# Hawk and RWKV layer on one core: three groups of entries moved in a hand-written order table

## The chip, the cores and the metric

The kernel runs on one core of one Trainium2 chip. The metric is the device time of one execution in microseconds (us). Shown times are the median of three runs; the profile is of one further execution.

## The reference

For 8 sequences of 1024 tokens and 256 channels, in float32, a block adds a recurrent layer (Hawk) and a channel mix (RWKV) to its input. Both read the normalised input.

```python
xn = layernorm(x)                                  # over the 256 channels
# Hawk, 384 hidden channels
gate, u = xn @ Wg.T, xn @ Wi.T
y = causal_depthwise_conv(u, conv_w) + conv_b      # 4 taps
ig = sigmoid(y @ lru_Wi.T + lru_bi)
rg = sigmoid(y @ lru_Wg.T + lru_bg)
alpha = exp(-8 * softplus(lam) * rg)
xbeta = sqrt(1 - alpha**2 + 1e-6) * ig * y
h = scan(h[t] = alpha[t] * h[t-1] + xbeta[t])
hawk = (gelu(gate) * h) @ Wo.T
# RWKV channel mix; x_prev is xn one token earlier
xr = mu_r * xn + (1 - mu_r) * x_prev
xk = mu_k * xn + (1 - mu_k) * x_prev
rwkv = sigmoid(xr @ W_r.T) * (relu(xk @ W_k.T)**2 @ W_v.T)
out = x + hawk + rwkv
```

## The kernel before

The kernel goes through the 8 sequences in 8 rounds, one sequence a round, with the work of neighbouring sequences laid over each other: while a round's matrix products run, the next sequence is normalised, turned and mixed, and the sequence before has its recurrence finished. All products are in float32 on tiles of 128 rows by 512 tokens (or, for r, v and o, four blocks of 128 tokens).

**Products in groups.** A pair of row blocks times two halves of the tokens would be four outputs of two products each. The class `Group` makes them with seven products in place of eight, from sums of weight blocks (`sum_u`, `sum_l`, ... made once on POOL, line 408) and differences of token halves (`xsum`, `ysum`, `rsum`, ... made each round on POOL, line 797). A group uses PSUM banks named A, B, C (and D where there is a third channel block) and runs in numbered steps on TensorE (lines 415 and 421):

- step 1: a product into A, one into C. ScalarE then copies A into B (`seed`, line 491) and C into an SBUF tile (`five`, line 496).
- step 2: A is completed and evicted as output (0,0); a product is added into B. VectorE then writes B + five into C (`fork_c`, line 499).
- step 3: a product is added into B, one into C. VectorE then writes B + five as output (1,1), for groups without a third block straight into the output's place (`fork_d`, line 507), followed by `late`, ScalarE's function on it in place; for the groups l into bank D. C is evicted as output (0,1).
- step 4: a last product is added into B, which needs fork d to have read B first; B is evicted as output (1,0). Step 5, with a third block only, completes D.

The groups are u0, u1, u2 (both input projections), l0, l1, l2 (both gates' projections of y), k, r, v, o. Their evictions differ: u goes to `u` by a copy (line 611) or to `g` by Gelu (line 615); l to `tr` and `ti` by Tanh (line 623); k by Relu (line 660) and, once both rows of a token half are there, Square (line 663) into the tile `ysum`, which is lent to the key; r by Tanh into `side` (line 675).

**The first round** differs: its first group is plain, v is four plain products with the key's squares (`v_product`, line 824) whose results VectorE multiplies with r (`value`, line 846), and the second sequence is normalised in it. For that, VectorE takes statistics of x (line 721 and 723, "second stats"), ScalarE takes the root (`deviation`, line 726, which needs a table of its own), VectorE the reciprocal and the scaled mean (`inverse`, lines 733 and 734), and ScalarE normalises eight tiles (`normalize`, line 743), which TensorE turns (line 748). VectorE also runs nine convolution steps (`conv_rest`, line 880), three for each third of `y`. The group l0 needs the thirds of y and, from POOL, the differences `ysum` of their halves.

**The second round** has at its end the statistics of the sequence after next (`stats`, lines 721 and 723). They read `xt`, which four DMAs on SP's queue fill (`load_for_squares`, line 717), issued behind sixteen DMAs that turn the normalised tiles into `xnT` (`spread`, line 786). VectorE there also finishes the mixed inputs `xk` and `xr` of the next sequence (`mix`, line 814; ScalarE has started them in `mix_before`, line 808), two channel blocks each. Of the mixed key POOL makes token differences into `side`.

**The order.** No scheduler is at work. TensorE's steps are called in the order wanted (`pe`, which advances a clock by the product count). All else is put down with `at`, whose time comes from the table `PLACES` where the step's name stands in it. At the end everything is sorted by time and issued in that order; each engine works through its own instructions strictly in it:

```python
        if name in places:
            t = base[0] + places[name]
        steps.append((t, len(steps), f, args, name))
...
        for _, _, f, args, _ in sorted(steps, key=lambda e: e[:2]):
            f(*args)
```

`PLACES` has one table for the first round, one for the second, one for the rounds in the middle and one for the last. Its numbers are counted in TensorE products from the round's start; only their order has an effect. A step's name is the group's, the function's and its arguments: "k evict B 1 0" is the key's eviction of bank B, "deviation" and "inverse 0 8" in the first table are the second sequence's root and scales, "mix k 1" is channel block 1 of the mixed key.

Of the kernel before, what the change touches and what calls it, by code (L numbers as in the profile page):

```python
# [60 lines left out]
        "u1 late": 27.8, "conv_rest 1 1": 28.18, "r five": 28.48, "conv_first 2": 29.16,  # L61
        "early token_sum r 1": 29.68, "u2 evict B 1 0": 30.51, "conv_rest 0 1": 30.84,
        "u1 evict B 1 0": 31.19, "u2 late": 31.87, "early token_sum r 2": 32.34, "k fork_d": 32.34,
        "early constant 2": 33.49, "early token_sum r 3": 33.63, "r fork_c": 33.77, "deviation": 33.9,
        "early constant 3": 34.38, "early weight_sum l 3 False": 34.51, "k evict B 1 0": 34.53,
        "inverse 0 8": 35.4, "early weight_sum l 2 False": 35.77, "r fork_d": 35.86, "k late": 36.28,
        "conv_rest 2 1": 36.43, "normalize 7 1": 36.67, "early weight_sum o 0 False": 37.83,
        "conv_rest 1 2": 38.21, "r evict B 1 0": 39.35, "early weight_sum v 2 False": 39.7,
        "k evict C 0 1": 40.03, "conv_rest 0 2": 40.08, "early weight_sum o 1 False": 41.29,
        "r evict A 0 0": 41.42, "conv_rest 0 3": 41.48, "r evict C 0 1": 42.02, "normalize 1 1": 42.7,  # L70
        "conv_rest 2 2": 42.96, "normalize 4 1": 43.4, "normalize 6 1": 44.1, "token_sum y 0": 44.45,
        "r late": 44.8, "normalize 2 1": 45.47, "conv_rest 1 3": 45.6, "l0 seed": 46.8,
        "conv_rest 2 3": 47.0, "l0 five": 47.65, "normalize 5 1": 48.29, "value 0": 48.34,
        "token_sum y 1": 48.34, "normalize 0 1": 48.93, "value 6": 49.06, "token_sum y 2": 49.38,
        "l0 evict A 0 0": 49.72, "value 2": 49.8, "normalize 3 1": 50.52, "token_sum y 3": 50.52,
        "l0 fork_c": 50.86, "value 4": 51.67, "early weight_sum v 0 False": 51.68, "l1 seed": 51.86,
# [55 lines left out]
        "v evict B 1 0": 57.82, "token_sum y 1": 57.82, "mix_before r 0": 57.85, "o evict C 0 1": 58.55,  # L132
        "mix_before r 1": 58.96, "token_sum y 3": 59.0, "token_sum y 2": 60.16, "l0 evict A 0 0": 60.18,
        "l0 fork_c": 60.36, "v late": 61.32, "token_sum x 0": 62.12, "l1 seed": 62.36,
        "token_sum x 2": 63.28, "l1 five": 63.36, "stats 7 1": 63.74, "token_sum x 1": 64.44,
        "l0 fork_d": 64.47, "stats 6 1": 65.28, "add_x": 65.61, "mix k 1": 66.01,
        "l0 evict C 0 1": 66.36, "decay 0": 67.3, "stats 0 1": 67.5, "token_sum x 3": 67.5,
        "stats 4 1": 68.23, "l0 evict B 1 0": 68.64, "mix k 0": 68.96, "decay_square 0": 69.44,
        "mix r 0": 70.46, "l1 evict A 0 0": 70.55, "token_sum k 0": 71.96, "l1 fork_c": 71.96,
# [1196 lines left out]
```

## Time and profile before

| what | value |
|---|---|
| median of 3 runs | 624.31 us (623.81 to 625.08) |
| the profiled execution: time | 624.13 us |
| the profiled execution: span from first to last instruction | 622.4 us |
| granted TensorE clock over the span | 1.00 |
| share of the chain that ended last: TensorE | 93% |
| same chain: VectorE, ScalarE, DMA | 3%, 2%, 1% |

Times inside the profile are counted from the start of the span. PE is TensorE's products, PEld its weight loads, DVE is VectorE, ACT is ScalarE, POOL is GpSimd, SP the queue that issues most DMAs. A row of the timeline gives start, duration, engine, line, operation, out<-in by the program's names, partitions by elements, the number of instructions run together, and in brackets the engine's idle time before them with what ended it. A row of the waits gives who waited, for whom, the sum in us, how often and the longest. A second name behind a bank tile says which operands: w_r,xr are the products of r. Instructions that follow on VectorE and ScalarE without a wait start about 0.1 us before the row ahead of them ends.

### The profile page before, as it was taken

The page shows a single profiled execution, that of the slowest core. Times are in us where ns is not written, and L with a number is a line of the kernel's source. Part 1 is how long each engine was busy: PE and PEld are TensorE (multiplying, and loading weights), DVE is VectorE, ACT ScalarE, POOL GpSimd, SP SyncE. Part 2 cuts the span into 40 slices and gives each one's busy share as a digit, 9 for nine tenths or more (in the row PEclk, how much of TensorE's full clock was granted, in tenths as well). Part 3 has the DMA queues.
Part 4 walks back from the last instruction along what each step waited for, and adds up shares of the span by engine and source line. Part 5 has one row for each costly group of instructions (what it writes and reads, how often), then busy time and mean ns, then how long its engine had stood idle before and what let it go on. Part 6 is the DMA issues. An engine that isn't in the chain of part 4 may idle for free.

```text
span 622.4 us, 7477 instructions
## 1 busy us (share of the span) xinstructions
PE 613.1 (99%) x2539; PEld 369.8 (59%) x2539; DVE 530.4 (85%) x656; ACT 473.1 (76%) x670; POOL 321.6 (52%) x227
## 2 busy tenths in 40 slices
PE   8999999999999999999999999999999999999997
PEld 4566445954459544695447844487445964457466
DVE  5788699989889898897889988998888987789695
ACT  4997998658985689847889398884888749883880
POOL 4996743667225870449506493084911769427000
PEclk9999999999999999999999999999999999999999
DMA  7200600064001730029000390006600044000403
GB/s 271 67 2 10 127 0 1 22 182 67 1 0 39 179 55 0 1 60 198 14 1 1 77 194 0 2 2 141 130 0 1 18 118 70 0 0 1 69 20 115
DMA packets 35334, 35.10 MB, mean 56 GB/s; under 512 B 2784, under 2 KB 34784, under 8 KB 35296
## 3 DMA queue, kind: packets, MB, share of 16 engines
q1 hardware_dynamic: 26560, 25.83, 15.1%
q0 software_dynamic: 8320, 8.39, 9.1%
q8 instruction: 20, 0.33, 0.2%
q10 hardware_dynamic: 416, 0.41, 0.2%
q14 instruction: 18, 0.15, 0.1%
HBM read 19.94 MB, written 8.39 MB: 46 GB/s over the span
## 4 chain that ended last, share of the span: by engine, by line
PE 93%; DVE 3%; ACT 2%; DMA 1%; issue 1%; DVEq 0%; ACTq 0%
PE bank L415 62%; PE bank L421 24%; PE bank L824 4%; PE bank L1007 1%; PE bank L581 1%; DMA out_dram<-side 1%; DVE q L897 1%; DVE xk L814 0%; DVE xr L814 0%; DVE st L721 0%; ACT g L615 0%; PE bank L748 0%; DVE bank L499 0%; PE bank L1026 0%; ACT L726 0%
## 5 line engine op out<-in xcount | busy, mean ns | idle before, releaser
L415 PE MATMUL bank<-y,w_l 128*128 128x512 f32 x288 | 137.9, 593 | 0.0
L880 DVE SCALAR_TENSOR_TENSOR y<-u,par,y 128x1024 f32<-128x1024 f32 x72 | 111.4, 1572 | 0.2
L491 ACT COPY bank<-bank 128x512 f32<-128x512 f32 x76 | 43.7, 576 | 62.4 <-PE bank L415 46.5
L415 PEld LDWEIGHTS bank<-y,w_l 128*128 128x128 f32 x288 | 53.0, 190 | 58.6 <-issue 57.3
L499 DVE TENSOR_TENSOR bank<-bank,five 128x512 f32<-128x512 f32 x76 | 52.3, 689 | 27.1 <-PE bank L415 25.5
L415 PE MATMUL bank<-ysum,sum_l 128*128 128x512 f32 x144 | 71.1, 593 | 0.2 <-DVE bank L499 0.2
L415 PE MATMUL bank<-xsum,sum_u 128*128 128x512 f32 x138 | 69.3, 592 | 0.0
L797 POOL TENSOR_TENSOR tr<-g 128x512 f32<-128x512 f32 x12 | 22.0, 1835 | 79.9 <-ACT u L611 69.3
L797 POOL TENSOR_TENSOR ysum<-y,ysum 128x512 f32<-128x512 f32 x16 | 28.5, 1779 | 52.4 <-DVE y L880 52.3
L797 POOL TENSOR_TENSOR xsum<-ysum 128x512 f32<-128x512 f32 x12 | 16.0, 1350 | 66.0 <-PE bank L421 58.8
L415 PEld LDWEIGHTS bank<-ysum,sum_l 128*128 128x128 f32 x144 | 26.9, 190 | 35.0 <-issue 28.2
L496 ACT COPY five<-bank 128x512 f32<-128x512 f32 x76 | 43.7, 583 | 5.1 <-PE bank L415 3.2
L415 PE MATMUL bank<-xnT,w_u 128*128 128x512 f32 x92 | 47.0, 592 | 0.0
L623 ACT ACTIVATE tr<-bank,half_b 128x512 f32<-128x512 f32 x48 | 32.1, 680 | 17.2 <-PE bank L415 17.2
L415 PEld LDWEIGHTS bank<-xsum,sum_u 128*128 128x128 f32 x138 | 25.7, 190 | 29.7 <-issue 27.5
L421 PE MATMUL bank<-w_o,g 128*128 128x128 f32 x288 | 37.0, 275 | 0.0
L623 ACT ACTIVATE ti<-bank,half_b 128x512 f32<-128x512 f32 x48 | 31.5, 683 | 7.1 <-PE bank L415 6.9
L421 PEld LDWEIGHTS bank<-w_o,g 128*128 128x128 f32 x288 | 35.0, 192 | 2.9 <-issue 2.9
L743 ACT ACTIVATE xt<-xt,mv,std 128x256 f32<-128x256 f32 x60 | 34.0, 596 | 1.7 <-DVE mv L734 1.7
L904 DVE SCALAR_TENSOR_TENSOR ti<-ti,y 128x1024 f32<-128x1024 f32 (+1 forms) x25 | 31.0, 1259 | 3.9 <-ACT ti L623 3.9
L797 POOL TENSOR_TENSOR ysum<-y 128x512 f32<-128x512 f32 x16 | 21.3, 1329 | 23.8 <-DVE y L880 23.8
L907 DVE SCALAR_TENSOR_TENSOR ti<-ti,q 128x1024 f32<-128x1024 f32 (+1 forms) x25 | 32.6, 1305 | 0.7
(164 smaller groups left out, 1476.7 us busy)
## 6 DMA issues: line engine op xcount, KB each, us to landing
side<-in_x_dram POOLq DMA_DIRECT2D x8, 1024.0 KB, 9.3
xt<-in_x_dram SPq DMA_DIRECT2D x28, 256.0 KB, 4.5
xnT<-xk SPq DMA_DIRECT2D x96, 64.0 KB, 2.0
out_dram<-side SPq DMA_DIRECT2D x12, 512.0 KB, 5.0
xt<-in_x_dram SPq DMA_DIRECT2D x1, 1024.0 KB, 5.5
out_dram<-side SPq DMA_DIRECT2D x4, 256.0 KB, 2.2
out_dram<-side SPq DMA_DIRECT2D x8, 128.0 KB, 1.7
w_l<-in_lru_wg_dram SPq DMA_DIRECT2D x1, 576.0 KB, 5.9
```

The lines of the kernel that those rows point to most:

```text
L415: nc.tensor.matmul(banks[b], weight, tokens, start=start, stop=True, skip_group_check=True)
L421: nc.tensor.matmul(banks[b][:, p], tokens[:, p], weight, start=start and j == 0, stop=True, skip_group_check=True,)
L491: nc.scalar.copy(banks[bank["B"]], banks[bank["A"]])
L496: nc.scalar.copy(self.five, banks[bank["C"]])
L499: nc.vector.tensor_tensor(banks[bank["C"]], banks[bank["B"]], self.five, ALU.add)
L623: nc.scalar.activation(dst[:, m, HALVES[h]], src, AF.Tanh, bias=half_b[:, b + m : b + m + 1], scale=0.5)
L743: nc.scalar.activation(xa, xa, AF.Identity, bias=m, scale=r)
L797: nc.gpsimd.tensor_tensor(dst[o], a, b, ALU.subtract)
L824: nc.tensor.matmul(banks[b][:, j * D : (j + 1) * D], lhs[:, c, (t + j) * P : (t + j + 1) * P], families[w][:, c, :], start=(j == 0 and c = ...
L880: nc.vector.scalar_tensor_tensor(y[:, m, :], u[:, m, k : k + S], column(COL_CONV_W + k * HC + m), y[:, m, :], ALU.mult, ALU.add,)
L904: nc.vector.scalar_tensor_tensor(ti[:, m, p], ti[:, m, p], 1.0, y[:, m, p], ALU.add, ALU.mult)
L907: nc.vector.scalar_tensor_tensor(ti[:, m, p], ti[:, m, p], 0.5, q[:, m, p], ALU.mult, ALU.mult)
```

## The change

Nothing is added and nothing left out. Entries of the table get other numbers, and so other places among the instructions of their engines.

First round: `deviation` goes from 33.9 to 40.1 and `inverse 0 8` from 35.4 to 41.0. On ScalarE the root, with the two table loads around it, so moves behind the key's eviction of B with its square, the key's late relu, r's eviction of B, and the key's eviction of C with its square. On VectorE the reciprocal and the scaled means move behind r's fork d and three of the convolution steps. `normalize 7 1`, `2 1` and `6 1` move with them: the first tile is normalised behind r's evictions of A and C, three others a little later than before.

Second round: `l0 fork_d` goes from 64.47 to 63.7 and `mix k 1` from 66.01 to 64.0, `stats 7 1` from 63.74 to 64.5. On VectorE fork d and mix k 1 so move ahead of `stats 7 1` and `stats 6 1`.

TensorE's, POOL's and SP's instructions keep their order, and so do the tables of the other rounds.

```diff
@@ table "first" @@
-        "early constant 2": 33.49, "early token_sum r 3": 33.63, "r fork_c": 33.77, "deviation": 33.9,
+        "early constant 2": 33.49, "early token_sum r 3": 33.63, "r fork_c": 33.77,
-        "inverse 0 8": 35.4, "early weight_sum l 2 False": 35.77, "r fork_d": 35.86, "k late": 36.28,
-        "conv_rest 2 1": 36.43, "normalize 7 1": 36.67, "early weight_sum o 0 False": 37.83,
-        "conv_rest 1 2": 38.21, "r evict B 1 0": 39.35, "early weight_sum v 2 False": 39.7,
-        "k evict C 0 1": 40.03, "conv_rest 0 2": 40.08, "early weight_sum o 1 False": 41.29,
-        "r evict A 0 0": 41.42, "conv_rest 0 3": 41.48, "r evict C 0 1": 42.02, "normalize 1 1": 42.7,
-        "conv_rest 2 2": 42.96, "normalize 4 1": 43.4, "normalize 6 1": 44.1, "token_sum y 0": 44.45,
-        "r late": 44.8, "normalize 2 1": 45.47, "conv_rest 1 3": 45.6, "l0 seed": 46.8,
-        "conv_rest 2 3": 47.0, "l0 five": 47.65, "normalize 5 1": 48.29, "value 0": 48.34,
+        "early weight_sum l 2 False": 35.77, "r fork_d": 35.86, "k late": 36.28, "conv_rest 2 1": 36.43,
+        "early weight_sum o 0 False": 37.83, "conv_rest 1 2": 38.21, "r evict B 1 0": 39.35,
+        "early weight_sum v 2 False": 39.7, "k evict C 0 1": 40.03, "conv_rest 0 2": 40.08,
+        "deviation": 40.1, "inverse 0 8": 41.0, "early weight_sum o 1 False": 41.29,
+        "r evict A 0 0": 41.42, "conv_rest 0 3": 41.48, "r evict C 0 1": 42.02, "normalize 7 1": 42.6,
+        "normalize 1 1": 42.7, "conv_rest 2 2": 42.96, "normalize 4 1": 43.4, "token_sum y 0": 44.45,
+        "r late": 44.8, "conv_rest 1 3": 45.6, "l0 seed": 46.8, "conv_rest 2 3": 47.0, "l0 five": 47.65,
+        "normalize 2 1": 47.7, "normalize 6 1": 48.0, "normalize 5 1": 48.29, "value 0": 48.34,
...
@@ table "second" @@
-        "token_sum x 2": 63.28, "l1 five": 63.36, "stats 7 1": 63.74, "token_sum x 1": 64.44,
-        "l0 fork_d": 64.47, "stats 6 1": 65.28, "add_x": 65.61, "mix k 1": 66.01,
+        "token_sum x 2": 63.28, "l1 five": 63.36, "l0 fork_d": 63.7, "mix k 1": 64.0,
+        "token_sum x 1": 64.44, "stats 7 1": 64.5, "stats 6 1": 65.28, "add_x": 65.61,
```

## The prediction

> **What bounds the kernel now.** The page's busy row came first, then the waits of TensorE, then the timeline around the two longest.
>
> ```profile
> PE 613.1 (99%) x2539; PEld 369.8 (59%) x2539; DVE 530.4 (85%) x656; ACT 473.1 (76%) x670; POOL 321.6 (52%) x227
> ```
>
> ```profile
> PE bank L415 <- DVE bank L507: 1.5, 1, 1.5
> ...
> PE bank L421 <- DVE side L507: 1.1, 1, 1.1
> ...
> PE bank L415 <- DVE bank L499: 0.2, 1, 0.2
> ```
>
> TensorE sets the end. A shorter kernel needs fewer TensorE waits, and only some 5 us of them exist. The two longest both wait for a fork d (L507): r's in the first round, l0's in the second. The change moves these two. The first:
>
> ```profile
> 40.36 1.28 ACT L726 ACT_TABLE_LOAD   x1
> ...
> 41.66 0.31 ACT L726 ACTIVATE std<-mv,ln_eps 128x8 f32<-128x8 f32 x1
> ...
> 42.00 0.20 DVE L733 RECIPROCAL std<-std 128x8 f32<-128x8 f32 x1 [1.43 <-ACT std L726]
> 42.23 0.80 DVE L734 SCALAR_TENSOR_TENSOR mv<-mv,std 128x8 f32<-128x8 f32 x1
> ...
> 42.96 0.68 DVE L507 TENSOR_TENSOR side<-bank,five 128x512 f32<-128x512 f32 x1
> ...
> 43.78 1.13 PE L421 MATMUL bank<-w_r,rsum 128*128 128x128 f32 x8 [1.12 <-DVE side L507]
> ```
>
> VectorE stands still for 1.43 until ScalarE has loaded a table and taken the root; fork d is queued behind, and TensorE behind fork d. The second:
>
> ```profile
> 133.95 1.68 DVE L686 SCALAR_TENSOR_TENSOR side<-side,five 128x512 f32<-128x512 f32 x1
> 137.77 0.43 DVE L721 BATCH_NORM_STATS2 st<-xt 128x6 f32<-128x256 f32 x1 [2.15 <-DMA xt<-in_x_dram]
> 138.24 0.18 DVE L723 BATCH_NORM_AGGREGATE mv<-st 128x2 f32<-128x6 f32 x1
> 138.34 0.67 DVE L507 TENSOR_TENSOR bank<-bank,five 128x512 f32<-128x512 f32 x1
> ...
> 139.06 1.12 PE L415 MATMUL bank<-ysum,w_l 128*128 128x512 f32 x2 [1.47 <-DVE bank L507]
> ```
>
> Here the row ahead of fork d waits for the load of x.
>
> **What covers the first stall.** In the first round VectorE has hardly any slack before the group l0, which needs convolution and token sums:
>
> ```profile
> 48.76 1.28 DVE L880 SCALAR_TENSOR_TENSOR y<-u,par,y 128x1024 f32<-128x1024 f32 x1
> 49.95 2.30 DVE L880 SCALAR_TENSOR_TENSOR y<-u,par,y 128x1024 f32<-128x1024 f32 x1
> ...
> 49.01 2.16 POOL L797 TENSOR_TENSOR ysum<-y 128x512 f32<-128x512 f32 x1 [3.77 <-DVE y L880]
> 52.42 2.16 POOL L797 TENSOR_TENSOR ysum<-y,ysum 128x512 f32<-128x512 f32 x1 [1.25 <-DVE y L880]
> ...
> 55.22 0.59 PE L415 MATMUL bank<-ysum,sum_l 128*128 128x512 f32 x1
> ```
>
> POOL and VectorE take turns: POOL's sum from 49.01 ends 1.13 after the convolution that ended at 50.04, and the convolution from 49.95 ends 1.09 after that sum. The last sum shown ends at 54.59, its product starts at 55.22.
>
> **First round, step by step.** No row of the work and no DMA is added or removed; SP's and POOL's queues keep their order. The old times hold until TensorE's stall.
>
> VectorE: B's last product for r ends at 41.77 (eight products after 40.64, issued 0.11 apart), after the key's own (40.61). Fork d starts 0.04 later, as the fork c at 66.77 does after its product, and ends at 42.49 (0.68). TensorE followed it by 0.14 (43.64 to 43.78), so it goes on at 42.63: 1.15 early.
>
> ScalarE: the key's eviction of B (0.58) starts at 40.65 rather than 41.87, its square (1.06) ends at 42.32, its late relu (0.61) at 42.83. The next in the queue is r's eviction of B. It waits for r's last group, which ended at 44.91 and now ends at 43.76. Behind it stand the key's eviction of C, a square, the table load and the root: 0.60, 0.59, 1.06, 1.28, 0.31, less 0.10 of overlap in one place and plus 0.05 of gaps. The root is there at 47.58, not 41.97.
>
> VectorE: three convolutions follow fork d. POOL's weight sums (42.01 to 45.24) may take turns with them, so they end between 46.3 (1.28 each) and 47.0. Neither decides: the reciprocal waits for the root anyway and starts at 47.60. Reciprocal 0.18, scales 0.17 (the row at 101.47, POOL idle; 0.80 at 42.23 beside a POOL row). The fourth convolution ends at 49.23, formerly 48.84: 0.39 late. The turns repeat behind it: first y sum 51.56 (51.17), second third of y 52.65, third 53.84, second y sum 54.98 (54.59).
>
> TensorE: four values (L824) and the first l0 product keep the 1.15. The first sum's product could start at 51.37, waits for 51.56 and starts at 51.62. y's second third lets it go on at 52.71 (53.40), the third at 53.90 (54.36), the second sum at 55.04. The product behind that one starts at 55.58; it was 55.65. Of 1.15, 1.08 are given back: **-0.1**. Bounds: -1.15 if the y chain comes no later than now; +0.6 if the scales take 0.80 again. I take the working's value, as POOL has nothing to do from 47.4 to 49.2.
>
> Two covers, on ScalarE: l0's seed had 1.30 of idle time before 52.77. r's two late evictions and three normalize steps now end at 51.95, so the seed ends at 52.44, ahead of 52.71. The normalize steps end at 56.4 (56.59), the transposes start at 60.3. If the seed's cover were gone, each microsecond would go to TensorE.
>
> **Second round.** Two instructions move ahead of two statistics pairs on VectorE: fork d and mix k 1. B's product (135.29, 0.59) ends at 135.88, and VectorE is free from 135.62. Fork d runs from 135.92 to 136.60, before TensorE wants it. TensorE's last product started at 137.01 and they go 0.43 apart, so the next starts at 137.44 rather than 139.06; as it then ran 0.70 instead of 0.59, the one behind gains 1.74.
>
> Mix k 1 waits for the spread of xnT, which ScalarE's rows on xk (131.94) have had, not for x. Its row was 2.29 beside a POOL row. It now ends at 137.84, after POOL's sum (135.02, 1.74) and 1.08 of its own. POOL's sum from 136.72 then ends near 139.0, a microsecond late; POOL's add_x DMA (137.93) and the last x sum slip likewise. Both are wanted some 17 us later at the earliest (the u products on xsum, 157.69).
>
> Next late could be l1's fork c (145.24 to 145.93), for TensorE comes for it at 144.3 (146.04 less 1.74). Ahead of it: four statistics pairs (0.53 each) from 137.8, mix k 0, mix r 0 (1.25, 1.28) and one POOL turn (1.1). They end near 143.3, fork c at 143.9: covered. l2's fork c ended at 154.10 and cost 0.44 (0.17 idle, a slow start, the lost cadence). VectorE gains some 2.0 there and TensorE 1.74, so 0.2 of it goes too. ScalarE keeps up: its 1.03 of waiting at 144.52 goes first. Sum **-1.9**; bounds -2.2 (all of the 0.44) and -1.3 (fork c half a microsecond late).
>
> **Sum.** The profiled execution took 624.13, 622.4 of span and 1.7 around it, 0.18 under the median of 624.31. Off it come 0.1 and 1.9: 622.1, on the median's scale 622.3.
>
> **Rivals.**
> The whole first stall is kept (-1.15 - 1.9: 621.2). For it: PE idle 1.12, DVE waiting 1.43. Against it: the root comes 5.6 later, and the y chain hangs on it.
>
> The first round loses (+0.6 - 1.9: 623.0), by scales beside a POOL row. For it: 42.23. Against it: POOL's queue is empty then.
>
> The second gain is halved (-0.1 - 0.9: 623.3): fork c or a wait of mix k 1 for x takes the stall over. For it: x lands at 137.7, and the DMA queues are shared. Against it: 0.4 of margin, and the spread was issued from 119.67, x from 130.49.
>
> A table switch costs more than its load, so the root comes later. Were each of the two to cost its load again (1.28), the root would come at 48.9 and the seed, behind both, end at 55.0 rather than 53.34: TensorE +1.7, in all 624.1, no change. Rows speak against it: the load ends at 41.64, the root starts at 41.66. The Trainium skill ("ScalarE: Activation LUTs", section "What ACT_TABLE_LOAD costs") states a drain of about 1380 ns beside a load of about 1283 ns; the trace agrees with the load (1283) and shows no drain here.
>
> Slower: weight sums of POOL slide into the four last convolutions. Each turn ahead of the second y sum costs 1.1; from two turns on the first round loses more (2.2 - 0.1) than the second gains (1.9). With two it is 624.5, with three 625.6. For it: such turns made the convolution at 36.44 take 2.29. Against it: by these rows the sums are done by 47.4.
>
> That the moves don't take place is excluded: the compiled order has both.
>
> **How the numbers follow.** Forecast 0.58, full gain 0.12, first round loses 0.13, second halved 0.08, table 0.03, slower 0.06. The range goes from the full gain to past the halved one: 621.0 to 623.8. A measurement tells 0.2% (1.25 us) from no change, so faster ends at 623.06: nearly all of the forecast, all of the full gain, half of the third, a little of the fourth: 0.74; same 0.19; slower 0.07.
>
> **What would show it.** In the first round TensorE's wait of 1.1 is gone and fork d ends near 42.5; the root ends near 47.6; VectorE idles ahead of the reciprocal; TensorE waits for y sums near 51.5 to 55, and stands at 60.3 about where it stood. In the second, fork d ends near 136.6 and TensorE has no idle time near 137 to 139. I am wrong if the root comes before 46 or after 49, or if a wait of over 0.5 for a fork c stands at 144 or 152.

## The result and the profile after

The changed kernel takes 622.28 us (median of 19 runs, 621.54 to 623.55), the one before 623.94 us in as many runs beside it (622.63 to 626.28; the 624.31 given ahead was the median of three of them). The ratio is 0.9978, with a 95% interval of 0.997 to 0.9986: about a fifth of a per cent faster. It is not the quotient of the two medians, which is 0.9973; nor, as a rule, are the ratios further down. The profiled execution spans 620.9 us against 622.4.

The waits of TensorE by the profile after (who waited, for whom, us in total, times, longest) answer to those of before:

```profile
...
PE bank L415 <- DVE bank L499: 0.4, 2, 0.3
...
```

Both waits for a fork d (L507: 1.1 and 1.5) are gone, 2.6 us in all, and yet the span is only 1.5 shorter. In their place the waits for a fork c (L499) have grown from 0.2 to 0.4. What more was given back doesn't stand there. In the first round, ScalarE and VectorE by the timeline of the changed kernel (start, us, engine, line, operation):

```profile
44.10 0.60 ACT L675 ACTIVATE side<-bank 128x512 f32<-128x512 f32 x1 [1.02 <-PE bank L421]
...
47.59 0.30 ACT L726 ACTIVATE std<-mv,ln_eps 128x8 f32<-128x8 f32 x1
...
42.10 0.69 DVE L507 TENSOR_TENSOR side<-bank,five 128x512 f32<-128x512 f32 x1 [1.31 <-PE bank L421]
42.71 4.41 DVE L880 SCALAR_TENSOR_TENSOR y<-u,par,y 128x1024 f32<-128x1024 f32 x3
47.93 0.20 DVE L733 RECIPROCAL std<-std 128x8 f32<-128x8 f32 x1 [0.81 <-ACT std L726]
...
48.25 5.88 DVE L880 SCALAR_TENSOR_TENSOR y<-u,par,y 128x1024 f32<-128x1024 f32 x4
```

Fork d runs when its product is done, ahead of the root. But the root is 5.9 us later than before, VectorE waits for it again with four convolution steps queued behind, and the last of them ends at 54.13 instead of 53.45. TensorE's rows of the same stretch:

```profile
42.94 1.13 PE L421 MATMUL bank<-w_r,rsum 128*128 128x128 f32 x8
...
51.90 1.12 PE L415 MATMUL bank<-ysum,sum_l 128*128 128x512 f32 x2
53.08 2.23 PE L415 MATMUL bank<-y,w_l 128*128 128x512 f32 x4
55.32 1.12 PE L415 MATMUL bank<-ysum,sum_l 128*128 128x512 f32 x2
```

The first row started at 43.78 before, the last at 55.22. The waits in between are so short that the modelled ends of the products hide them: they show as rows that start later than 0.43 per product, not as idle time.

The second round, VectorE and TensorE of the changed kernel:

```profile
135.75 0.70 DVE L507 TENSOR_TENSOR bank<-bank,five 128x512 f32<-128x512 f32 x1 [0.29 <-PE bank L415]
136.36 1.32 DVE L814 SCALAR_TENSOR_TENSOR xk<-xnT,par,xk 128x1024 f32<-128x1024 f32 x1
137.60 0.41 DVE L721 BATCH_NORM_STATS2 st<-xt 128x6 f32<-128x256 f32 x1
...
139.73 2.97 DVE L814 SCALAR_TENSOR_TENSOR xk<-xnT,par,xk 128x1024 f32<-128x1024 f32 x1
142.63 1.27 DVE L814 SCALAR_TENSOR_TENSOR xr<-xnT,par,xr 128x1024 f32<-128x1024 f32 x1
143.82 0.69 DVE L499 TENSOR_TENSOR bank<-bank,five 128x512 f32<-128x512 f32 x1
...
137.27 1.02 PE L415 MATMUL bank<-ysum,w_l 128*128 128x512 f32 x2
...
144.56 1.13 PE L415 MATMUL bank<-ysum,sum_l 128*128 128x512 f32 x2 [0.27 <-DVE bank L499]
```

Fork d and mix k 1 fill the time in which VectorE waited for x, and TensorE passes 137.27 without a stop. Seven microseconds on it waits for l1's fork c, held up by a mix k 0 of 2.97.

**One table for all kernels.** Profiled executions differ mostly in their first 16 us (see the end), so spans alone mislead. For this table I read when the same product starts in two kernels, beginning at r's step 3 in the first round (40.64 in the kernel before), and note by how much the distance to the kernel before changes from each place to the next (minus is earlier than before). The places are the second product on l0's second y sum (55.65 before), the second of r's step 3 in the second round (110.11), and the second products behind l0's fork d (139.60), l1's fork c (146.52) and l2's fork c (154.69). The changed kernel has them at 55.85, 109.94, 137.70, 145.10 and 153.27, and starts at 40.86, 0.22 late: 55.85 - 55.65 - 0.22 is -0.02, and so on. Behind the last place the lead stays within 0.02 to the end of the kernel.

| kernel | start | first round | to 110 | l0's fork d | l1's fork c | l2's fork c | sum without start |
|---|---|---|---|---|---|---|---|
| changed kernel | +0.22 | -0.02 | -0.37 | -1.73 | +0.48 | 0.00 | -1.64 |
| first round's moves only | +0.23 | -0.01 | -0.23 | -0.52 | +0.52 | -0.01 | -0.25 |
| second round's moves only | +0.23 | 0.00 | -0.02 | -1.74 | +0.49 | 0.00 | -1.27 |
| fork d of l0 alone | +0.03 | -0.01 | 0.00 | -1.74 | +1.75 | -0.01 | -0.01 |
| changed, add_x late | -1.41 | -0.02 | -0.37 | -1.74 | -0.05 | -0.44 | -2.62 |
| changed, root early | -0.95 | -0.70 | -0.01 | -1.74 | +0.49 | -0.01 | -1.97 |
| changed, inverse last | -1.52 | -1.02 | +0.03 | -1.74 | +0.48 | 0.00 | -2.25 |
| root early, add_x late | -1.42 | -0.69 | -0.37 | -1.74 | -0.05 | -0.44 | -3.30 |
| inverse last, add_x late | -0.25 | -1.03 | +0.03 | -1.74 | -0.06 | -0.44 | -3.23 |

### The profile page after: what moved, and what is told of

Read it like the earlier page. It is cut to its first block, busy times and chain, and to the rows that moved or that the text cites. A ratio compares the mean times of both kernels' runs of the same rounds, so it can differ in the third digit from the quotient of the medians.

```text
span 620.9 us, 7479 instructions
## 1 busy us (share of the span) xinstructions
PE 613.7 (99%) x2539; PEld 369.7 (60%) x2539; DVE 530.2 (85%) x656; ACT 472.5 (76%) x670; POOL 325.8 (52%) x227
## 4 chain that ended last, share of the span: by engine, by line
PE 92%; POOL 3%; DVE 2%; ACT 1%; issue 1%; DVEq 0%; POOLq 0%
PE bank L415 62%; PE bank L421 24%; PE bank L824 3%; POOL xsum L797 1%; PE bank L1007 1%; POOL side L797 1%; POOL rsum L797 1%; DVE q L897 1%; PE bank L581 0%; POOL sum_l L408 0%; DVE xr L814 0%; POOL ysum L797 0%; DVE st L721 0%; PE bank L748 0%; POOL w_v L394 0%
## 5 line engine op out<-in xcount | busy, mean ns | idle before, releaser
L499 DVE TENSOR_TENSOR bank<-bank,five 128x512 f32<-128x512 f32 x76 | 52.3, 689 | 26.6 <-PE bank L415 25.5
```

Of the source, the lines that this page charges most:

```text
L499: nc.vector.tensor_tensor(banks[bank["C"]], banks[bank["B"]], self.five, ALU.add)
```

## The experiments

All edits are numbers in the order table. The edits are shown against the changed kernel. Ratios are to the kernel before, run beside each on the same chip, with the 95% interval.

**The first round's moves only.**

```diff
 "second": (as before)
-        "l0 fork_d": 63.7, "mix k 1": 64.0, "stats 7 1": 64.5
+        "l0 fork_d": 64.47, "mix k 1": 66.01, "stats 7 1": 63.74
```

> Only the first round's moves; the second round as before. Theory (the late root hands the gain back through the y chain): r's fork d ends near 42.8 and TensorE's wait of 1.1 there is gone, the root ends near 47.9, and from the second l0 token sum (about 55.3) on TensorE stands within 0.3 us of before; the stall of 1.5 at l0's fork d in the second round is there in full; time within 0.5 us of before (0.2 us shorter if the token-sum turn at 107 also goes VectorE's way). Rival (the first stall's 1.1 us is kept): TensorE is 1.0 to 1.1 us ahead at 55 and at 137, and the time is 1.1 us shorter.

Measured 623.3 us, ratio 0.9998 (0.9988 to 1.0008). Of the stall's 1.1, 0.01 is left at the second y sum. The stall at l0's fork d was not there in full, as the theory had it, but 0.9 long: in this execution x landed earlier, and VectorE's first statistic starts at 137.24 rather than 137.77. It made no odds, since l1's fork c took the 0.52 back: mix k 1, behind the statistics here, takes 2.81 rather than 2.29 and ends at 141.86, as before (141.87). Both times that is 1.09 behind the end of POOL's last x sum (140.77; 140.78).

**The second round's moves only.**

```diff
 "first": (as before)
-        "deviation": 40.1, "inverse 0 8": 41.0, "normalize 7 1": 42.6, "normalize 2 1": 47.7, "normalize 6 1": 48.0
+        "deviation": 33.9, "inverse 0 8": 35.4, "normalize 7 1": 36.67, "normalize 2 1": 45.47, "normalize 6 1": 44.1
```

> Only the second round's moves; the first as before. Theory (the second round carries the change): the first stall of 1.1 stands, the second is gone, l1's fork c takes back 0.4 to 0.5, time 1.2 to 1.3 us shorter than before. Rival (the two rounds share the gain): 0.6 us or less.

Measured 622.31 us, ratio 0.9975 (0.9963 to 0.9987), which is what the whole change gives. The first stall stands at 1.1, l0's fork d gives 1.74, l1's fork c takes 0.49: the theory holds. By the table this kernel is 0.37 short of the changed one, nearly all of it in a step before 110 that neither group of moves aims at (see the next section).

**l0's fork d alone.**

```diff
 "first": (as before)
 "second":
-        "mix k 1": 64.0, "stats 7 1": 64.5
+        "mix k 1": 66.01, "stats 7 1": 63.74
```

> Only l0's fork d is moved, mix k 1 stays behind the two statistics. Theory (fork d frees TensorE at once, but mix k 1 has to fill VectorE's wait for x, else l1's fork c is late): TensorE gains 1.7 at l0's fork d and gives about 0.9 back at l1's fork c, which ends near 145.2; time 0.8 us shorter than before. Rival (mix k 1 doesn't matter, or even harms by taking turns with POOL): 1.3 to 1.7 us shorter.

Measured 623.66 us, ratio 0.9997 (0.9986 to 1.0007): neither theory had this. All of the 1.74 comes back as a wait for l1's fork c:

```profile
138.19 0.43 DVE L721 BATCH_NORM_STATS2 st<-xt 128x6 f32<-128x256 f32 x1 [1.56 <-DMA xt<-in_x_dram]
...
139.40 2.50 DVE L814 SCALAR_TENSOR_TENSOR xk<-xnT,par,xk 128x1024 f32<-128x1024 f32 x1
...
137.96 1.54 POOL L851 DMA_DIRECT2D side<-in_x_dram  x1
138.91 1.90 POOL L797 TENSOR_TENSOR xsum<-xnT,xsum 128x512 f32<-128x512 f32 x1
...
145.27 0.69 DVE L499 TENSOR_TENSOR bank<-bank,five 128x512 f32<-128x512 f32 x1
...
146.02 1.13 PE L415 MATMUL bank<-ysum,sum_l 128*128 128x512 f32 x2 [1.54 <-DVE bank L499]
```

VectorE still waits for x (1.56 in these rows of its timeline), and mix k 1 then takes 2.50. Fork c starts at 145.27, as it did at 145.24 with the stall in place. I had counted on 0.7 us, fork d's own length, for it. Part of it was lost as x landed later in this execution (138.19; 137.77), the rest in mix k 1, which takes 2.50 rather than 2.29: it started at 139.58 before, at 139.40 here and at 139.05 in the kernel with the first round's moves only, and each time ended 1.09 behind POOL's sum, whose row here ends at 140.81. So behind the statistics it is this sum, more than the load of x, that sets when mix k 1 is done. The move of mix k 1 is what makes the move of fork d worth anything: it fills VectorE's wait for x, and it takes mix k 1 out from behind this sum. The runs do not part these two effects.

**POOL's add_x behind the last x sum.** Why did mix k 0 take 2.97? POOL's timeline in the changed kernel:

```profile
138.76 1.55 POOL L851 DMA_DIRECT2D side<-in_x_dram  x1
139.71 1.90 POOL L797 TENSOR_TENSOR xsum<-xnT,xsum 128x512 f32<-128x512 f32 x1
```

The sum starts 0.02 before mix k 0 (139.73) but lies partly behind the DMA's issue, which lasts to 140.31. It ends at 141.61, and mix k 0 ends 1.09 after it. It is the same sum that mix k 1 met in the kernels above.

```diff
 "second":
-        "add_x": 65.61
+        "add_x": 67.6
```

> The changed kernel with POOL's add_x DMA of the second round moved behind the last x token sum. Theory (POOL's sum, issued behind the DMA's 1.55 us, holds the port that mix k 0 wants, so the turn costs 1.9 in place of 1.1): mix k 0 is done a microsecond or more earlier (2.97 falls under 1.8), l1's fork c ends before TensorE comes for it, and the wait of 0.3 there is gone: 0.4 to 0.5 us shorter than the changed kernel. Rival (VectorE's own four statistics and two mixes make fork c late): no change, the wait at l1's fork c stays.

Measured 620.91 us, ratio 0.9964 (0.995 to 0.9979). With the DMA out of its way the two last x sums run from 134.93 to 138.53 together, the last one in 1.27 rather than 1.90, and VectorE does this:

```profile
138.10 1.51 DVE L814 SCALAR_TENSOR_TENSOR xk<-xnT,par,xk 128x1024 f32<-128x1024 f32 x1
139.53 1.27 DVE L814 SCALAR_TENSOR_TENSOR xr<-xnT,par,xr 128x1024 f32<-128x1024 f32 x1
140.73 0.68 DVE L499 TENSOR_TENSOR bank<-bank,five 128x512 f32<-128x512 f32 x1
```

Mix k 0 takes 1.51, and l1's fork c ends at 141.41, ahead of TensorE, which comes at 142.5. The wait is gone (-0.05 in place of +0.48), as the theory said. The edit does two things at once: the sum is shorter, and it comes earlier, so that mix k 0 meets only its end. l2's fork c, which had cost 0.44 in every kernel so far, costs nothing either, which I had not expected of this edit. The rows show why: from l1's fork c to l2's VectorE takes 8.17 before (145.24 to 153.41), 8.17 in the changed kernel and 8.18 here, so l2's fork c is early where l1's is.

**The root early.** The root stays where it was before; the reciprocal and scales follow r's fork d directly. The key's eviction of C moves too, and the three normalize steps stay where the change put them.

```diff
 "first":
-        "deviation": 40.1, "inverse 0 8": 41.0, "k evict C 0 1": 40.03
+        "deviation": 33.9, "inverse 0 8": 35.9, "k evict C 0 1": 36.5
```

> The changed kernel, but the root stays early as before and only the reciprocal and scales move, directly behind r's fork d; the key's eviction of C goes ahead of r's eviction of B, so that the values' squares are early enough. Theory (the late root, not the move of fork d, hands the first round's gain back): root near 42, y's thirds 0.2 us earlier than before instead of 0.6 later, TensorE keeps 0.7 to 0.9 of the 1.1 past the second y sum's product, 0.7 us shorter than the changed kernel. Rival (the first round's y chain is bound by VectorE and POOL whatever the root does): TensorE stands within 0.2 us of the changed kernel at that product.

Measured 621.43 us, ratio 0.9971 (0.9959 to 0.9983). TensorE keeps 0.70 of the 1.1, so the theory holds for the first round. By the table the kernel is 0.33 ahead of the changed one and not the 0.7 expected, since it has not the 0.37 before 110.

**The inverse behind the convolution.** The root as late as in the changed kernel, but with nothing of y queued behind it.

```diff
 "first":
-        "inverse 0 8": 41.0, "normalize 7 1": 42.6, "normalize 1 1": 42.7, "normalize 4 1": 43.4,
-        "normalize 6 1": 48.0, "normalize 5 1": 48.29, "normalize 0 1": 48.93
+        "inverse 0 8": 47.1, "normalize 7 1": 47.66, "normalize 1 1": 47.67, "normalize 4 1": 47.68,
+        "normalize 6 1": 49.73, "normalize 5 1": 49.74, "normalize 0 1": 49.75
```

> The changed kernel with the reciprocal and scales behind all convolution steps of the first round, and the normalize steps behind l0's five and eviction of A: the root comes as late as in the changed kernel, but nothing of the y chain is queued behind it. Theory (VectorE's wait for the root is what is late): VectorE's idle time before the reciprocal is gone, the second y sum ends near 54.1 instead of 55.3, TensorE keeps 0.9 to 1.1 us at its product. Rival (turns with POOL alone make the y chain late): it ends within 0.3 us of 55.3 and nothing is kept.

Measured 621.42 us, ratio 0.9964 (0.9951 to 0.9978). VectorE's timeline (this execution runs 1.7 ahead of the changed one's from the start):

```profile
40.36 0.69 DVE L507 TENSOR_TENSOR side<-bank,five 128x512 f32<-128x512 f32 x1 [1.31 <-PE bank L421]
40.96 10.42 DVE L880 SCALAR_TENSOR_TENSOR y<-u,par,y 128x1024 f32<-128x1024 f32 x7
51.31 0.19 DVE L733 RECIPROCAL std<-std 128x8 f32<-128x8 f32 x1
```

All seven convolution steps run through and the reciprocal waits for nothing. TensorE keeps 1.02, nearly all that the stall was worth. POOL still takes its turns here, so they are not what gave the gain back: what stood ahead of the fourth step was, in the changed kernel 0.81 of waiting for the root and 0.32 for the reciprocal and scales (47.93 to 48.25).

**Both remedies, in two ways.** First the early root with add_x late, then the inverse last with add_x late; the edits are those above, together.

> The early root of the first round together with the late add_x DMA of the second. Theory (both waits that took gains back are separate): both gains add, no wait on VectorE is left on TensorE in the first two rounds beyond 0.2, time 1.6 to 1.9 us shorter than the changed kernel, 3.2 to 3.5 shorter than before. Rival (a later stage takes the second gain back): no more than with add_x late alone, 1.0 us shorter than the changed kernel.

Measured 620.24 us, ratio 0.9947 (0.9934 to 0.9961): the gains add, and the table has 3.30.

> The reciprocal and scales behind all convolution steps of the first round, and add_x behind the last x token sum of the second. Theory (the two give-backs have separate causes, and both are now gone): TensorE keeps 1.0 in the first round, 1.7 at l0's fork d and another 0.4 to 0.5 at l2's fork c, so counted from the start of the first round's products it is 3.1 to 3.3 ahead of before; 1.3 to 1.5 us shorter than the changed kernel. Rival (with all else faster, another engine takes over in a later round): less than 2.8 ahead, and a new wait stands in TensorE's rows.

Measured 619.94 us, ratio 0.994 (0.9926 to 0.9954): 0.6% faster than the kernel before, where the change brought 0.2%. By the table it is 3.23 ahead of before where the changed kernel is 1.64 ahead, a little more than the 1.3 to 1.5 between them that were expected. TensorE's waits hold nothing of VectorE's but the start:

```profile
PE bank L1007 <- DVE five L984: 1.2, 1, 1.2
PE bank L581 <- ACT xnT L1039: 0.5, 2, 0.3
PE bank L421 <- POOL rsum L797: 0.2, 1, 0.2
```

The two kernels with both remedies are not told apart from each other by their intervals.

## Why the prediction was right, and where it was wrong

The time was forecast at 622.3 and came out at 622.28, but a match this close is luck. The forecast took 2.0 off a median of 624.31; beside the changed kernel the one before took 623.94, so by the medians 1.66 came off, and by the table 1.64. The steps behind the 2.0 are not all right either: some 0.75 less was gained than they say (0.08, 0.48 and 0.2 in the list below), and 0.37 came that no step had.

- **First round, -0.1:** measured -0.02. Fork d's end (42.49 forecast, 42.79 measured), the root's (47.58; 47.89) and the late convolution all came as worked out to within 0.1, once the 0.22 of a later start is taken off. That the late root, with the convolution queued behind it, is the cause is shown twice: root early keeps 0.70, inverse last keeps 1.02.
- **l0's fork d, -1.74:** measured -1.73, and the same in every kernel that moves it.
- **l1's fork c "covered":** this step failed. It cost 0.48. The term that was mis-sized is the "one POOL turn (1.1)" ahead of it: mix k 0 waited 1.88 of its 2.97 for POOL's sum (139.73 to 141.61), as the sum itself lay behind the DMA's issue, and so took 1.7 more than the 1.25 counted for its own work. Moving the DMA away removes the wait. The prediction had named a wait of over 0.5 here as a sign of being wrong; 0.48, of which 0.27 shows as idle time, is just short of it.
- **l2's fork c, -0.2:** measured 0.00. It hung on VectorE's gaining 2.0 against TensorE's 1.74. VectorE gained 1.42 at both fork c (145.24 to 143.82, 153.41 to 151.99), which by then was just what TensorE had gained.
- **Not forecast: -0.37 before 110.** In the second round's early part VectorE's scan got its turn ahead of a POOL sum that had come first in the kernel before. VectorE's and POOL's timelines, before:

```profile
106.93 2.32 DVE L912 TENSOR_TENSOR_SCAN q<-tr,q,ti 128x512 f32<-128x512 f32 x1
...
106.90 1.27 POOL L797 TENSOR_TENSOR xsum<-ysum,xsum 128x512 f32<-128x512 f32 x1
```

and after:

```profile
107.14 1.28 DVE L912 TENSOR_TENSOR_SCAN q<-tr,q,ti 128x512 f32<-128x512 f32 x1
...
107.19 2.29 POOL L797 TENSOR_TENSOR xsum<-ysum,xsum 128x512 f32<-128x512 f32 x1
```

Who comes 0.03 or 0.05 us first takes the turn, and the other's row is a microsecond longer. The scan stands ahead of r's fork c, which starts at 108.35 rather than 109.17, and so TensorE gains. The scan comes first in four kernels of the table (changed, first round's moves only, which loses 0.14 on the way there, add_x late, root early with add_x late) and second in the other five. In the four, POOL's sum just ahead of this one takes 1.36 to 1.38 rather than 1.27, which makes POOL late. The edit alone does not decide it: "root early" and "root early, add_x late" have the same instructions up to add_x, 30 us later, and the first has -0.01 here, the second -0.37. So this 0.37 can't be credited to the moves; without it the change brings 1.27, as the second round's moves alone do.

Of the rivals, that the whole first stall is kept fell with the first experiment, and the table switch that costs more than its load fell with the changed kernel's rows: the load from 46.30 ends at 47.58, the root starts at 47.59 and the next load follows at 47.91. "The second gain is halved" was the nearest: fork c did take over, though by a quarter of the gain, and not because of a wait for x.

## What to carry to other kernels

Before an instruction is moved out of a stalled queue, look at what its engine does next: l0's fork d alone was worth nothing, as VectorE's next work still waited for x and for POOL, and with one more instruction moved ahead of both waits it was worth 1.3 us. A stall that is moved behind other work has to be followed to the next consumer of that work: here the root took from the convolution what it had cost fork d. And where two engines take turns, the price of a turn is not the other engine's instruction alone but also what that instruction still waits behind.

## What was not expected of the hardware

**A turn got longer where the other engine's instruction lay behind a DMA issue.** A turn is the wait of one engine while the other's instruction has its row: VectorE's mix of 139.73 waited for POOL's sum, recorded from 139.71 to 141.61, though POOL's DMA issue lasted until 140.31. The mix took 2.97 rather than 1.27; in the turn at 107 the scan took 2.32 rather than 1.28. The sum's row is 1.90 behind the DMA and 1.27 with the DMA moved away, so some 0.6 of it, as much as the two rows overlap (139.71 to 140.31), looks like waiting. That the sum keeps VectorE out in that time is read from the rows alone, and rows on POOL are rough; no run tests it.

**Profiled executions differ by up to 1.7 us before r's step 3.** TensorE's lead there, the table's first column, goes from -1.52 to +0.23, which is as much as the whole change brings. A part comes from the fifteen warm-up products that open TensorE's timeline. They start 0.43 apart and go over to 0.22 apart at some moment, which differs from one execution to the next (behind the product that starts at 4.14 at the earliest, at 6.70 at the latest), so that the last of them starts between 5.70 and 6.94. The rest arises behind them, and what decides it was not tested. The runs of one kernel scatter by 1.4 to 3.7 us; how much of that comes from the start was not measured.
